# Two-layer adaLN block on one core: each attention maximum placed behind the next reciprocal of row 0's Sinkhorn chains

## The chip, the cores and the metric

The kernel runs on one core of one Trainium2 chip. A core has five engines that work side by side, each from its own list of instructions and in the order of that list: TensorE (PE; PEld is its weight load), VectorE (DVE), ScalarE (ACT), GpSimd (POOL) and SyncE (SP), which here issues the DMAs. An instruction that waits for another engine holds up everything behind it in its own list. The metric is the time of one execution on the device in microseconds, the median of several.

## The reference

Two transformer layers work on `x` of shape (2, 512, 512): two rows (batch entries, `b`) of 512 tokens. Each layer normalises, modulates, runs an attention, then normalises, modulates and runs a second part. Layer 0 is a large gated linear attention (32 heads of 128) and a binarised matrix product; it takes the first 850 us and the change does not touch it. Layer 1 is a softmax attention with 32 heads of 16, and after it a mixing of four streams of 128 channels whose 4x4 mixing matrix comes from a Sinkhorn iteration:

```python
def step(carry, _):
    u, v = carry
    u = -jax.nn.logsumexp(Z + v[..., None, :], axis=-1)
    v = -jax.nn.logsumexp(Z + u[..., :, None], axis=-2)
    return ((u, v), None)
(u, v), _ = jax.lax.scan(step, (u0, v0), None, length=50)
H_res = jnp.exp(Z + u[..., :, None] + v[..., None, :])
```

A token has 16 logits `Z`; 50 iterations of a row step and a column step follow each other, every step a function of the one before. The softmax of the attention is `softmax(q k / 4)` over 512 keys, and its result is added to `x` before the mixing reads it.

## The kernel before

Tokens lie 128 to a tile, so a row has four tiles and there are eight in all.

Attention of layer 1. It is cut into 16 groups (`order`, two rows x two halves of the queries x four head groups), each in 8 pieces. `piece()` runs through them. For each piece `maxima` makes two maxima: a matmul of scores for 128 queries by 512 keys into a PSUM buffer (L880; the pool `s1` has three) and a reduction to the row's negated maximum on VectorE (L884). After four pieces' share of them (8 maxima) the maxima are split in a high and a low part (L894 on ScalarE, L895 on GpSimd), turned on TensorE (L898) and written by a DMA (L904) as extra rows of the queries. Some ten pieces later `weigh` computes the scores again in the turned layout, with the maximum subtracted inside the matmul (L918), and ScalarE takes the exponential (L78, `pt`). `outputs` multiplies by the values (L938), `finish` turns, divides and adds to `x` (L960, L964, L966 and on GpSimd L972). There are 256 maxima, numbered 0 to 255 here.

Sinkhorn chains. When a quarter of the tokens (half a row, two tiles) has its attention, a generator for its mixing goes onto the list `side`, which `piece()` advances by two steps a piece (`aside(2)`). For row 0 that is `streams0(0)` and `streams0(2)`: `opening` (normalisation and logits), `first_iteration`, 49 further `iterations` and the mixing. For row 1 `streams1a` runs 16 iterations of the first half, `streams1b` then opens the second half, runs 33 iterations of both halves together ("joint") and 16 more of the second half alone.

A chain keeps `K = exp(Z + u + v)` and two factors `fa` and `fb`. A half iteration multiplies `K` by one factor, sums over four, and takes the reciprocal:

- row 0: the product (L1183 or L1187) and the sum in two additions (L1176, L1177) on GpSimd, the reciprocal (L1185 or L1189) on VectorE, 98 reciprocals a chain;
- row 1 (`last` is true): product, sum (L1173) and reciprocal all on VectorE, 130 reciprocals.

At iterations 16 and 32 of a run (`RENEW`) the factors are folded into `u` and `v` and `K` is computed anew (L1193, L1166, L1167 on VectorE, logarithms and the exponential on ScalarE). At the end `result` forms the matrix (L1200, L1201, L1204), ScalarE makes diagonal matrices of its entries (L1215), TensorE mixes (L1236), and `put` scales and adds (L1210 on VectorE, L1211 on GpSimd) and stores.

Order. The order of each engine's list is not the order of the text. A scheduler places every instruction by priorities (`tc.high_priority` moves work forward) and by its own estimate of when operands are ready. `tc.add_manual_dep(a, b, order_only)` adds a rule: `a` stands behind `b` in their engine's list; where both are on one engine it puts no semaphore between them. In the resulting list VectorE had 64 of the first chain's 98 reciprocals, 28 of the second's and 2 of row 1's 130 ahead of the last maximum.

Of the kernel before, what the change touches and what calls it, by code (L numbers as in the profile page):

```python
# [52 lines left out]
def tile_adaln(ctx: ExitStack, tc: tile.TileContext, a: dict, out: bass.AP):  # L53
    nc = tc.nc
# [22 lines left out]
    def act(o, i, func, **kw):  # L77
        ins = nc.scalar.activation(o, i, func, **kw)  # L78
        tc.add_manual_dep(
            ins.ins, table.ins.name,  # L80
            mybir.DependencyInfo(mybir.DependencyClass.NoSync, mybir.DependencyReason.DATA),
            reason="the activation table",
        )
        return ins.ins
# [52 lines left out]
    anchor = {}  # L137
    order_only = mybir.DependencyInfo(mybir.DependencyClass.NoSync, mybir.DependencyReason.DATA)
# [32 lines left out]
    def temp(shape, dt, name, bufs=2):  # L171
        return wk.tile(shape, dt, name=name, bufs=bufs)
# [642 lines left out]
    def key_tile(i):  # L815
        return i % 2 if i < TWO else (i - TWO + 2) % 3
# [54 lines left out]
    def maxima(st, k):  # L871

        assert holder[key_tile(st["i"])] == st["i"]
        rp, j = divmod(k, 4)
        s, i = divmod(j, 2)
        if j == 0:
            st["m"] = small.tile([P, NQ * 2, 2], FP, name="m")
        for qt in range(NQ):
            ps = psp.tile([P, L], FP, name="s1", bufs=S1)
            anchor["pe"] = nc.tensor.matmul(  # L880
                ps, lhsT=st["qs"][rp][0:KS, i, qt * P:(qt + 1) * P], rhs=st["ks"][s][0:KS],
                start=True, stop=True,
            ).ins
            anchor["dve"] = nc.vector.tensor_reduce(  # L884
                st["m"][:, 2 * qt + s, i:i + 1], ps, AX.X, ALU.max, negate=True
            ).ins
        if j == 3:
            m2 = small.tile([P, NQ * 2, 2, 2], FR, name="m2")
            hi, lo = m2[:, :, 0], m2[:, :, 1]
            if st is order[-1]:  # L890
                nc.vector.tensor_copy(hi, st["m"])
                nc.vector.tensor_tensor(lo, st["m"], hi.bitcast(FP), ALU.subtract)
            else:
                nc.scalar.copy(hi, st["m"])  # L894
                nc.gpsimd.tensor_tensor(lo, st["m"], hi.bitcast(FP), ALU.subtract)  # L895
            mt = psp.tile([8, Q], FP, name="mt", bufs=MT)
            for qt in range(NQ):
                nc.tensor.transpose(  # L898
                    mt[:, qt * P:(qt + 1) * P],
                    m2[:, 2 * qt:2 * qt + 2].bitcast(FP).rearrange("p a b c -> p (a b c)"), ident,  # L900
                )
            mm = temp([8, L], FR, "mm")[:, 0:Q]
            nc.scalar.copy(mm, mt)
            anchor["sp"] = nc.sync.dma_start(out=st["qs"][rp].bitcast(FP)[96:100], in_=mm.bitcast(FP)).ins  # L904

    def weigh(st, k):

        assert holder[key_tile(st["i"])] == st["i"]
        rp, r = divmod(k, 4)
        kp, s = divmod(r, 2)  # L910
        if r == 0:
            quads.append({"st": st, "rp": rp, "pt": {}})
        qd = quads[-1]
        for i in range(2):
            ps = psp.tile([P, 2, Q], FP, name="s2", bufs=S2)
            for j in range(2):
                kt = 2 * kp + j
                nc.tensor.matmul(  # L918
                    ps[:, j, :], lhsT=st["ks"][s][0:KM, kt * P:(kt + 1) * P], rhs=st["qs"][rp][0:KM, i, :],
                    start=True, stop=True,  # L920
                )
            p = wts.tile([P, 2, Q], FP, name="pt", bufs=PT)
            anchor["act"] = qd["last"] = act(p, ps, AF.Exp, scale=0.25)
            qd["pt"][2 * s + i, kp] = p

    quads = []

# [232 lines left out]
    def iterations(R, its, renew, last):  # L1160

        z, t, K, u, v, fa, fb, fl = (R[k] for k in ("z", "t", "K", "u", "v", "fa", "fb", "fl"))
        big = nc.vector if last else nc.gpsimd

        def kernel_of():
            nc.vector.tensor_tensor(K, z, over(u), ALU.add)  # L1166
            nc.vector.tensor_tensor(K, K, along(v), ALU.add)  # L1167
            act(K, K, AF.Exp)

        def sums(dst, y):  # L1170

            if last:
                nc.vector.tensor_reduce(dst, y, AX.X, ALU.add)  # L1173
            else:
                h2 = R["pairs"]
                nc.gpsimd.tensor_tensor(h2, y[:, :, :, 0:2], y[:, :, :, 2:4], ALU.add)  # L1176
                nc.gpsimd.tensor_tensor(dst, h2[:, :, :, 0], h2[:, :, :, 1], ALU.add)  # L1177

        for it in its:
            if it == 1 or it - 1 in renew:  # L1180
                sums(fa, K)
            else:
                big.tensor_tensor(t, K, along(fb), ALU.mult)  # L1183
                sums(fa, t)
            nc.vector.reciprocal(fa, fa)  # L1185
            yield
            big.tensor_tensor(t, tp_(K), along(fa), ALU.mult)  # L1187
            sums(fb, t)
            nc.vector.reciprocal(fb, fb)  # L1189
            if it in renew:  # L1190
                for d, f in ((u, fa), (v, fb)):
                    act(fl, f, AF.Ln)
                    nc.vector.tensor_tensor(d, d, fl, ALU.add)  # L1193
                kernel_of()
            yield
# [70 lines left out]
    def streams0(c0):  # L1266

        S = {"b": 0, "c0": c0, "n": 2}
        yield from opening(S, False)
        R = chain_room(2, False)  # L1270
        yield from first_iteration(S, R)
        yield from S["branch"]
        yield from iterations(R, range(1, NITER), RENEW, False)
        result(S, R)
        for c in range(2):
            yield from mixed_on_tensor(S, c, nc.gpsimd)
# [3 lines left out]
    def streams1a():  # L1280

        S = joint["a"] = {"b": 1, "c0": 0, "n": 2}
        yield from opening(S, True)
        R = joint["R"] = chain_room(4, True)
        yield from first_iteration(S, part(R, 0, 2))
        yield from S["branch"]
        yield from iterations(part(R, 0, 2), range(1, HEAD + 1), (HEAD,), True)

    def streams1b(ahead):
# [16 lines left out]

        side.append((1, branches(), UP))
        yield from iterations(R, range(1, NITER - HEAD), RENEW, True)
        result(A, part(R, 0, 2))
        side.append((None, mixed_on_tensor(A, 0, nc.gpsimd), UP))  # L1310
# [44 lines left out]
    def piece():  # L1355
        p = at[0]
        at[0] += 1
        if p == 0:
            begin()
        i, k = divmod(p, 8)  # L1360
        if k == 0 and i < len(order):
            load_step(i + 1)
        if p < n_pieces:
            maxima(order[i], k)
        if wt[0] <= p - slack(p):
            weighed()
        if k == 4 and i + 1 < len(order):
            keys1(i + 1)
        with tc.high_priority(UP):
            if p >= HOLD and p % POP == 0 and virtual:  # L1370
                tail(virtual.pop(0))
        aside(2)
# [3 lines left out]
    def weighed():  # L1376
        w = wt[0]
        wt[0] += 1
        if w < n_pieces:
            if w == n_pieces // 2:  # L1380
                values1(1)
            weigh(order[w // 8], w % 8)
        o = w - OUT
        if 0 <= o < n_pieces and o % 4 == 3:
            outputs(o // 4)
        o -= 5
        if o >= 0 and o % 4 == 0 and o < n_pieces:
            j = o // 4
            finish(j)
            if j % 16 == 5:  # L1390
                with behind():
                    row_tiles(j // 16, (SB, CB, GB))
                    weights24(j // 16)
            if j % 8 == 7:
                k = j // 8
                if k == 2:
                    joint["ahead"] = streams1a()
                side.append((RATES[k], (streams0(2 * k) if k < 2 else joint["ahead"] if k == 2 else streams1b(joint["ahead"])), UPS[k]))
# [40 lines left out]
    for n, u in enumerate(units):  # L1439
        g, b, c = u["at"]  # L1440
        s = n // NC
# [127 lines left out]
```

## Time and profile before

| | us |
|---|---|
| median of 3 runs (1355.14 to 1362.71) | 1359.68 |
| profiled execution | 1362.77 |
| its span | 1361.1 |
| first and last maximum start | 854.6, 1224.4 |
| first chain of row 0: first and last reciprocal | 1081.1, 1275.7 |
| second chain of row 0: first and last reciprocal | 1159.1, 1323.4 |
| row 1's chain: first and last reciprocal | 1217.0, 1347.2 |

Over the span TensorE is busy 91%, VectorE 81%, ScalarE 62% and GpSimd 58%; the mean granted clock of TensorE is 0.961. In the lines that follow, a row of stages gives for each engine the busy time and the number of instructions, then the granted clock of TensorE (PEclk), the share of the DMA engines and what they moved. A row of the timeline gives start, length, engine, line, operation, what is written and read, and the count. A group gives busy time, mean length of one in ns, and after the second bar the idle time ahead of them and what ended it.

### The profile page before, as it was taken

The numbers are of one execution on the slowest core, as the hardware profiler recorded it, in microseconds if no ns is written. First come the engines' busy times: TensorE is split into PE (matmuls) and PEld (weight loads), VectorE is DVE, ScalarE is ACT, GpSimd is POOL, SyncE is SP. The second block draws the span as 40 slices with busy tenths as digits, with TensorE's granted clock in tenths as the row PEclk, the third lists the DMA queues.
The fourth block names the chain that finished last, engine by engine and source line by source line (L and its number), as shares of the span: only waits on it lengthen the run. The fifth ranks groups of instructions, "written<-read, shape, count | busy, mean of one in ns | idle before, by whom it ended". The sixth has DMA issues, their size and how long they took to land. (4 is left out here: it accounts for less than half of the span.)

```text
span 1361.1 us, 23047 instructions
## 1 busy us (share of the span) xinstructions
PE 1236.3 (91%) x7216; PEld 996.9 (73%) x7216; DVE 1098.5 (81%) x2668; ACT 845.2 (62%) x2380; POOL 788.3 (58%) x1235
## 2 busy tenths in 40 slices
PE   6889999999999999999989999898999999995408
PEld 3677888788788778888877787676777777764308
DVE  7897678787686687877989887867878888898888
ACT  4565476476466566766657675566667678775417
POOL 5353374365266357776788878444444755668751
PEclk9999999999999999999999999998998999997659
DMA  8111341231132142333343233424203221200001
GB/s 255 57 57 32 97 121 40 71 109 55 46 95 93 54 139 95 86 108 93 101 125 109 82 113 91 127 71 132 81 28 116 81 68 50 66 14 2 9 8 47
DMA packets 69762, 109.68 MB, mean 81 GB/s; under 512 B 13436, under 2 KB 20348, under 8 KB 69640
## 3 DMA queue, kind: packets, MB, share of 16 engines
q1 hardware_dynamic: 69640, 108.21, 26.9%
q8 instruction: 57, 0.93, 0.3%
q14 instruction: 65, 0.53, 0.1%
HBM read 99.89 MB, written 8.02 MB: 79 GB/s over the span
## 5 line engine op out<-in xcount | busy, mean ns | idle before, releaser
L884 DVE TENSOR_REDUCE m<-s 128x1 f32<-128x512 f32 x256 | 165.7, 670 | 13.6 <-PE s L880 13.0
L78 ACT ACTIVATE pt<-s 128x512 f32<-128x512 f32 x256 | 137.6, 600 | 13.4 <-PE s L918 12.6
L78 ACT ACTIVATE sg<-sg 128x512 f32<-128x512 f32 x128 | 80.8, 632 | 57.9 <-DVE sg L512 56.0
L481 POOL TENSOR_TENSOR q<-xcos,rot 128x512 f32<-128x512 f32 x64 | 92.9, 1452 | 39.7 <-DVE xcos L479 36.9
L880 PE MATMUL s<-ks,qs 96*128 96x512 f32 x256 | 105.1, 438 | 8.4 <-DVE m L884 6.2
L251 PE MATMUL pps<-hh,wq_h 128*128 128x512 f32 x256 | 102.0, 399 | 0.9 <-DVE zl L605 0.9
L78 ACT ACTIVATE dec<-dec,room 128x128 f32<-128x128 f32 x256 | 82.7, 398 | 32.1 <-POOL dec L529 31.9
L529 POOL TENSOR_SCALAR_AFFINE_SELECT dec<-gb 128x512 f32<-128x512 f32 x64 | 47.1, 736 | 95.6 <-DMA gb<-g_dram 35.1
L251 PE MATMUL ops<-wo_h,zh 128*128 128x512 f32 x256 | 101.3, 396 | 0.9 <-DVE zl L605 0.9
L251 PE MATMUL ops<-wo_h,zl 128*128 128x512 f32 x256 | 100.8, 394 | 0.9 <-DVE zl L605 0.9
L251 PE MATMUL gps<-wg_h,hh 128*128 128x512 f32 x256 | 101.1, 395 | 0.0
L251 PE MATMUL gps<-wg_l,hh 128*128 128x512 f32 x256 | 101.0, 394 | 0.0
L918 PE MATMUL s<-qs,ks 100*128 100x256 f32 x512 | 99.3, 301 | 1.7 <-ACT pt L78 1.2
L251 PE MATMUL gps<-wg_h,hl 128*128 128x512 f32 x256 | 100.6, 393 | 0.0
L251 PE MATMUL pps<-hl,wq_h 128*128 128x512 f32 x256 | 100.3, 392 | 0.0
L251 PE MATMUL ops<-wo_l,zh 128*128 128x512 f32 x256 | 100.1, 391 | 0.0
L251 PE MATMUL pps<-hh,wq_l 128*128 128x512 f32 x256 | 100.1, 391 | 0.0
L549 POOL TENSOR_TENSOR gb<-gb,q 128x512 f32<-128x512 f32 x48 | 63.2, 1318 | 63.1 <-ACT gb L78 52.2
L582 PE MATMUL yps<-v,dec 128*128 128x128 f32 x512 | 93.8, 278 | 3.8 <-DVE xcos L479 2.8
L918 PEld LDWEIGHTS s<-qs,ks 100*128 100x128 f32 x512 | 83.0, 195 | 18.0 <-ACT pt L78 5.3
L592 DVE SCALAR_TENSOR_TENSOR z<-yps,ss,sg 128x128 f32<-128x128 f32 x256 | 71.8, 341 | 28.4 <-ACT ss L78 28.1
L556 POOL TENSOR_TENSOR xw<-v,room 128x512 f32<-128x512 f32 x48 | 55.5, 1171 | 60.4 <-ACT v L496 58.1
(327 smaller groups left out, 3924.5 us busy)
## 6 DMA issues: line engine op xcount, KB each, us to landing
gb<-g_dram SPq DMA_DIRECT2D x64, 256.0 KB
raw<-in_wq SPq DMA_DIRECT2D x56, 256.0 KB
raw<-in_wg SPq DMA_DIRECT2D x48, 256.0 KB
raw<-in_wo SPq DMA_DIRECT2D x48, 256.0 KB
raw<-in_wmod SPq DMA_DIRECT2D x40, 256.0 KB
qs<-q_dram SPq DMA_DIRECT2D x64, 64.0 KB
raw<-in_wk SPq DMA_DIRECT2D x14, 256.0 KB
raw<-in_wv SPq DMA_DIRECT2D x14, 256.0 KB
```

What stands on the lines that cost most here:

```text
L78: ins = nc.scalar.activation(o, i, func, **kw)
L251: nc.tensor.matmul(ps, lhsT=l, rhs=r, start=i == 0, stop=i == n - 1)
L481: nc.gpsimd.tensor_tensor(dst, sp(xc_), sp(rot), ALU.add)
L529: anchor["pool"] = nc.gpsimd.affine_select(out=dec, in_=gb, pattern=[[0, REP0], [1, P]], compare_op=ALU.is_ge, fill=-1e30, base=0, channel ...
L549: nc.gpsimd.tensor_tensor(gb, gb, q[:, c], ALU.mult)
L556: nc.gpsimd.tensor_tensor(xw, u["v"][:, c, :].unsqueeze(1).to_broadcast(sh4), wdc[:, c, r0:r0 + REP0].unsqueeze(2).to_broadcast(sh4), ALU. ...
L582: nc.tensor.matmul(yps[:, h, :], lhsT=u["pr"][:, h, :], rhs=u["v"][:, c, :], start=True, stop=not c)
L592: nc.vector.scalar_tensor_tensor(z[:, h, :], yps[:, h, :], ss[:, h:h + 1], sg[:, h * P:(h + 1) * P], ALU.mult, ALU.mult)
L880: anchor["pe"] = nc.tensor.matmul(ps, lhsT=st["qs"][rp][0:KS, i, qt * P:(qt + 1) * P], rhs=st["ks"][s][0:KS], start=True, stop=True,).ins
L884: anchor["dve"] = nc.vector.tensor_reduce(st["m"][:, 2 * qt + s, i:i + 1], ps, AX.X, ALU.max, negate=True).ins
L918: nc.tensor.matmul(ps[:, j, :], lhsT=st["ks"][s][0:KM, kt * P:(kt + 1) * P], rhs=st["qs"][rp][0:KM, i, :], start=True, stop=True,)
```

## The change

Every reciprocal of a chain that has its products on GpSimd is noted in `paced`, a list for each chain. When a maximum is emitted, `pace` takes the next noted reciprocal from each list and demands that the maximum stand behind it. A rule concerns the order of VectorE's list alone. Nothing else is edited; the scheduler places all instructions anew under these rules.

```diff
             anchor["dve"] = nc.vector.tensor_reduce(
                 st["m"][:, 2 * qt + s, i:i + 1], ps, AX.X, ALU.max, negate=True
             ).ins
+            pace(anchor["dve"])
...
+    paced = {}
+
+    def pace(m):
+
+        for q in paced.values():
+            if q:
+                tc.add_manual_dep(m, q.pop(0).name, order_only, reason="the chain's reciprocals keep pace")
...
-            nc.vector.reciprocal(fa, fa)
+            r = nc.vector.reciprocal(fa, fa).ins
+            if not last:
+                paced.setdefault(id(R), []).append(r)
             yield
             big.tensor_tensor(t, tp_(K), along(fa), ALU.mult)
             sums(fb, t)
-            nc.vector.reciprocal(fb, fb)
+            r = nc.vector.reciprocal(fb, fb).ins
+            if not last:
+                paced[id(R)].append(r)
```

The lines behind the edits move: L884 stays, L1183, L1185, L1187 and L1189 become L1192, L1194, L1198 and L1200, L1176 and L1177 become L1185 and L1186.

## The prediction

> **What bounds the kernel now.** I read the page first (TensorE busy 91% of the span), then the busy time by stages, because the change touches only the last 280 us:
>
> ```profile
> core 0: us, PE busy (x) PEld busy (x) DVE busy (x) ACT busy (x) POOL busy (x), PEclk, DMA share, GB/s
> 1100.00:1120.00 20.00, 20.00 (x194) 14.79 (x190) 16.96 (x45) 15.33 (x35) 9.62 (x42) 1.00 0.18 50
> 1242.00:1256.00 14.00, 3.10 (x18) 2.74 (x18) 12.80 (x84) 4.58 (x17) 12.36 (x53) 0.57 0.00 1
> 1256.00:1276.00 20.00, 3.92 (x16) 3.25 (x15) 17.86 (x100) 3.55 (x13) 17.26 (x90) 0.50 0.00 0
> 1300.00:1324.00 24.00, 0.00 (x0) 0.00 (x0) 21.04 (x111) 0.69 (x3) 13.86 (x61) 0.50 0.00 1
> ```
>
> The attention (maxima until 1224.4) is bound by TensorE: PE is busy 20.00 of 20 us. After it PE is all but idle, and VectorE works through row 1's Sinkhorn chain, with row 0's two chains on GpSimd (POOL) between its instructions. The groups of 1100 to 1200 give the attention's pace:
>
> ```profile
> L884 DVE TENSOR_REDUCE m<-s 128x1 f32<-128x512 f32 x110 | 70.6, 666 | 9.3 <-PE s L880 9.0
> ```
>
> 110 maxima in 100 us, 0.91 us each. Next the timeline inside the attention, one half iteration of row 0's first chain (L1185 and L1189 are the reciprocals, L1187, L1176, L1177 its three GpSimd steps, L884 a maximum):
>
> ```profile
> 1152.05 0.19 DVE L1185 RECIPROCAL sinkhorn<-sinkhorn 128x8 f32<-128x8 f32 x1
> ...
> 1152.24 0.64 DVE L884 TENSOR_REDUCE m<-s 128x1 f32<-128x512 f32 x1
> 1152.32 0.25 POOL L1187 TENSOR_TENSOR sinkhorn<-sinkhorn 128x32 f32<-128x32 f32 x1
> ...
> 1152.65 0.22 POOL L1176 TENSOR_TENSOR sinkhorn<-sinkhorn 128x16 f32<-128x16 f32 x1
> ...
> 1152.95 0.20 POOL L1177 TENSOR_TENSOR sinkhorn<-sinkhorn 128x8 f32<-128x8 f32 x1
> 1152.97 0.68 DVE L884 TENSOR_REDUCE m<-s 128x1 f32<-128x512 f32 x1
> ...
> 1153.77 0.68 DVE L884 TENSOR_REDUCE m<-s 128x1 f32<-128x512 f32 x1
> ...
> 1154.37 0.19 DVE L1189 RECIPROCAL sinkhorn<-sinkhorn 128x8 f32<-128x8 f32 x1
> ```
>
> GpSimd is done at 1153.15, but the reciprocal stands behind two more maxima and starts at 1154.37: a half iteration takes 2.32 us here, and the chain is late, not the attention. The same steps with no maxima about, from the timeline of the tail, when row 0's second chain is alone on GpSimd:
>
> ```profile
> 1302.66 0.20 DVE L1189 RECIPROCAL sinkhorn<-sinkhorn 128x8 f32<-128x8 f32 x1
> ...
> 1303.55 0.20 POOL L1177 TENSOR_TENSOR sinkhorn<-sinkhorn 128x8 f32<-128x8 f32 x1
> ...
> 1303.79 0.20 DVE L1185 RECIPROCAL sinkhorn<-sinkhorn 128x8 f32<-128x8 f32 x1
> ...
> 1304.93 0.20 DVE L1189 RECIPROCAL sinkhorn<-sinkhorn 128x8 f32<-128x8 f32 x1
> ```
>
> 1.13 and 1.14 us; (1307.30 - 1302.66) / 4 = 1.16 over four. That is the chain's own speed, and it is slower than the 0.91 us of a maximum.
>
> **The change, part by part.** No instruction is added or removed. Each maximum gets the next reciprocal of each chain then at hand ahead of it in VectorE's list. Counted in the two built orders: of the first chain's 98 reciprocals, 64 stood ahead of the last maximum, now all 98; of the second's 98, 28, now 97; of row 1's 130, 2, now 23. Maxima 96 to 159 alternate one to one with the first chain, 160 to 191 with both, 192 to 255 with the second. VectorE takes its list in order, so a maximum now waits for GpSimd. Behind it wait the matmuls L880 that need its PSUM buffer (three), behind those in PE's list the scores L918 and outputs L938, and then ScalarE's exponentials: the whole attention falls to the chain's pace.
>
> (1) The pace. 128 steps with one chain at 1.16 us are 148.5. With two chains the tail shows the first chain's L1189 at 1262.32 and again at 1272.98, eight half iterations later: 1.33 us; 32 steps are 42.6. Together 191 us. A maximum itself (0.65) and the small VectorE work fit between two reciprocals, and PE's 0.91 lies inside the 1.16; both cost nothing as long as the step is longer. Bounds: 1.13 a step (the shortest row) below; above, 1.41 and 1.50, the means inside the attention (29 half iterations of the first chain from 1100 to 1160, and 27 of the second from 1160 to 1225) from a reciprocal's start to the end of its last sum, with GpSimd's other work included. I take 1.16 and 1.33 and list that other work:
>
> (2) Head: six GpSimd steps of row 1's rotary work (L702, L708) stand between the first half iterations; reciprocals 2 to 4 were at 1082.25, 1087.06 and 1091.08, so about 6 us over two normal steps. (3) The second chain's opening puts four 128x512 operations on GpSimd (L1061, L1062: 2.8 and 2.5 us); the half iteration over them took 5.9 us (1137.9 to 1143.80), 4.5 over a step. (4) Renewals: two in each chain; reciprocal 1148.19 to 1152.05 is 3.9, about 1 of it behind maxima, so 1.7 over a step; four make 7. (5) Every 8 maxima GpSimd adds an output (L972, 0.46) and a remainder (L895, 0.20): 20 x 0.66 = 13, half of it in the chain's own waits: 6. (6) Row 1's first 21 half iterations now stand among the last 25 maxima, some 0.6 us of VectorE a step beside 0.72 for maximum and reciprocal; 1.4 in place of 1.16: 7. (7) The first chain's mixing (40 diagonals on ScalarE at 0.29, two L1210 at 0.7, two adds on GpSimd) now lies among maxima 192 to 204: 4. Sum of 2 to 7: 34.5; from half of it to all.
>
> The first reciprocal was at 1081.07, with maxima 96 to 101 ahead of it; they now stand behind it, and four of them stood in the first iteration: about 1079. So the last maximum starts at 1079 + 191 + 34.5 = 1304.5, where it was at 1224.4: +80.
>
> (8) The tail. From the last maximum to row 1's joint iterations 31 us pass (1224.4 to 1256), set by the last exponentials, the last outputs and the second half's opening; it stays. But the second chain's mixing, 40 diagonals of 0.29 = 12 us of ScalarE, moves from 1324 into this drain, where ScalarE was busy 15.8 of 22 us, and its L1210 stands on VectorE ahead of the last outputs: +9 (0 if ScalarE finds room, 12 if not). Then row 1's 66 joint half iterations took 1256 to 1322.4 = 66.4 us beside row 0's chains; alone one is 0.80 (reciprocals at 1280.58 and 1281.38, while the second chain waits for a renewal): 53, and 5 for the joint chain's own two renewals, so -8, the stalls on row 0's results at 1284 to 1291 included. The tail is +1, between -15 (no drain, and every joint step at the 0.70 of the narrower steps after 1324) and +5.
>
> Reorderings of at most 36 places in the first 100 us come from the scheduler; the work is the same and PE is full there (100.00 of 100): 0, within 3. SP's list moves by at most 10 places (the last stores by 31); its queue loads L846 and copies L904 are the same number, spread over a longer stage, with the DMA share at 0.18: 0.
>
> Sum: +80 + 1 = +81. The profiled execution took 1362.8 (span 1361.1), 3.1 above the median 1359.68 of the runs shown; so 1362.8 + 81 - 3.1 = 1441.
>
> At this pace PE is busy about 0.91 / 1.4 = 65%. The rows show what can happen to its clock: 0.57 granted where PE was busy 22%, 1.00 where 85% (1220 to 1242), 0.96 at 60% (the last 14 us), 0.82 in 1081 to 1100. I take 1.00: at 0.8 PE's 0.91 becomes 1.14 at most and still lies inside the step.
>
> [...]
>
> **The rivals.**
> Not slower: the chain keeps pace with the attention because a waiting reciprocal was all that slowed it. For it: 23 of the first chain's 29 half iterations from 1100 to 1160 lose 0.4 us or more behind maxima. Then the last maximum stays at 1224 and the tail gives -8 to +1: 1352 to 1361. It decides where the 160 steps end 8 us late at most, (1232 - 1079) / 160 = 0.96 us a step; the shortest way from a reciprocal through GpSimd to the next is 1.13 in the rows shown, so I give it 2%.
> Cheap: the extras hide in each other and the tail gains its full 15. 128 x 1.13 + 32 x 1.25 + 17 = 202, last maximum at 1279: +55 - 15 = +40, 1400. For it: many extras are single waits that VectorE's slack can take.
> Dear: waits add up because each list is in order on five engines and two stand in a loop (the remainder L895 waits for ScalarE, which waits for maxima): 128 x 1.41 + 32 x 1.50 + 24 = 252, PE late 10: last maximum at 1341, +117, tail +5: 1482. A cooled PE belongs here.
> Nothing happens: the order shows that the lists differ; only an attention that waits for something else at 1.2 us anyway would hide it, and PE at 100% speaks against that.
>
> **How the numbers follow.** Forecast (1415 to 1465): 0.61. Cheap (1383 to 1415): 0.16. Dear (above 1465): 0.19. Not slower: 0.02. Nothing: 0.02. The range takes in most of cheap and dear: 1396 to 1485. Faster by over 0.5% 0.02, within 0.5% (what a measurement of this kernel can tell from no change) 0.02, slower 0.96.
>
> **What would show it.** The last maximum between 1280 and 1340; the attention's maxima at 1.2 to 1.5 us each; idle time before L1194 and L1200 (the reciprocals' new lines) put down to GpSimd's L1186, in place of few us now; PE busy 60 to 75% from 1100 on; no reciprocal of row 0's chains later than 5 us after the last maximum; 66 joint half iterations in 56 to 62 us. It is wrong if maxima run faster than 1.1 us, which a GpSimd part under 1 us would need, or if the tail shrinks by more than 20.

## The result, and the profile after

The changed kernel takes 1440.68 us (median of 6 runs, 1439.24 to 1442.68) where the kernel before takes 1360.23 (6 runs, 1355.14 to 1362.71): 1.0592 times as long, 95% interval 1.0571 to 1.0614. Its profiled execution took 1440.46, with a span of 1438.7, so 77.6 us more span than before.

The page of the kernel after: the span, the granted clock of TensorE in 40 slices (36 us each), and the group of the maxima (count, busy time and mean of one, then the idle time of VectorE ahead of them).

```profile
span 1438.7 us, 23052 instructions
...
PEclk9999999999999999999999999999998778988656
...
L884 DVE TENSOR_REDUCE m<-s 128x1 f32<-128x512 f32 x256 | 165.3, 659 | 10.1 <-PE s L880 10.1
```

Up to 1079 us the digit is 9 (0.9 or more) in every slice; from there to 1295 it is 7 or 8 in all but one of six. The busy time by stages of the kernel after (length, then busy time and instructions of each engine, granted clock, DMA share, GB/s):

```profile
core 0: us, PE busy (x) PEld busy (x) DVE busy (x) ACT busy (x) POOL busy (x), PEclk, DMA share, GB/s
1074.30:1311.10 236.80, 196.17 (x1401) 130.35 (x1405) 168.52 (x570) 132.76 (x340) 155.87 (x648) 0.84 0.12 35
...
1311.00:1345.00 34.00, 23.00 (x228) 18.26 (x220) 18.33 (x78) 22.37 (x69) 7.13 (x11) 0.89 0.04 16
1345.00:1401.00 56.00, 7.94 (x44) 7.20 (x44) 48.24 (x214) 9.74 (x36) 0.00 (x0) 0.56 0.00 1
```

The first row is the stretch from maximum 96 to the last one, 255. The same stretch of the kernel before:

```profile
1062.90:1224.40 161.50, 158.10 (x1370) 118.67 (x1370) 144.33 (x424) 122.73 (x302) 101.67 (x354) 0.98 0.22 59
```

161.5 us became 236.8. The stretch also begins 11.4 us later than in the kernel before, since maximum 96 now stands behind the first chain's first reciprocal, and what follows the last maximum is 9.1 us shorter: 11.4 + 75.3 - 9.1 = 77.6. TensorE's matmuls in the stretch are nearly the same (1401 and 1370), but it was short of work for 40.6 us of it (3.4 before), and was busy 38 us longer with them, at a mean clock of 0.84 in place of 0.98. No engine is full any more: the 159 maxima stand 1.49 us apart. In the last row GpSimd has nothing left: row 0's chains are done, and row 1's joint half iterations run alone. Two of these, from the timeline of the kernel after:

```profile
1349.51 0.25 DVE L1200 RECIPROCAL sinkhorn<-sinkhorn 128x16 f32<-128x16 f32 x1
1350.31 0.25 DVE L1194 RECIPROCAL sinkhorn<-sinkhorn 128x16 f32<-128x16 f32 x1
```

0.80 us. Below, the timeline of the kernel after where maxima and the first chain alternate:

```profile
1106.33 0.20 DVE L1194 RECIPROCAL sinkhorn<-sinkhorn 128x8 f32<-128x8 f32 x1 [0.60 <-POOL sinkhorn L1186]
1106.45 0.64 DVE L884 TENSOR_REDUCE m<-s 128x1 f32<-128x512 f32 x1
1106.61 0.25 POOL L1198 TENSOR_TENSOR sinkhorn<-sinkhorn 128x32 f32<-128x32 f32 x1 [0.32 <-DVE sinkhorn L1194]
...
1107.23 0.20 POOL L1186 TENSOR_TENSOR sinkhorn<-sinkhorn 128x8 f32<-128x8 f32 x1
1107.46 0.20 DVE L1200 RECIPROCAL sinkhorn<-sinkhorn 128x8 f32<-128x8 f32 x1 [0.38 <-POOL sinkhorn L1186]
1107.58 0.64 DVE L884 TENSOR_REDUCE m<-s 128x1 f32<-128x512 f32 x1
```

One half iteration, 1.13 us, and one maximum in it. The maximum is done at 1107.09; VectorE then idles 0.38 us for GpSimd's second addition, and the next maximum stands behind that. The waits of the kernel after between 1074 and 1311 (engine and line, what it waited for, us in total, times, longest):

```profile
DVE sinkhorn L1194 <- POOL sinkhorn L1186: 24.7, 49, 2.6
DVE sinkhorn L1200 <- POOL sinkhorn L1186: 23.1, 50, 2.1
...
PE s L880 <- DVE m L884: 15.6, 24, 2.1
PE s L919 <- DMA qs<-mm: 11.2, 10, 2.4
DVE m L884 <- PE s L880: 9.1, 8, 2.1
```

The same waits in the kernel before between 1081 and 1224:

```profile
DVE m L884 <- PE s L880: 11.2, 14, 1.8
...
DVE sinkhorn L1185 <- POOL sinkhorn L1177: 3.7, 6, 1.1
...
PE s L880 <- DVE m L884: 1.0, 3, 0.4
...
DVE sinkhorn L1189 <- POOL sinkhorn L1177: 0.2, 1, 0.2
```

The two waits for L1186 are the forecast's: 47.8 us, where the kernel before has 3.9 (6.4 over its whole span). The third line shows how the attention falls to the chain's pace: TensorE's scores wait for the maxima, 15.6 us for 1.0. The last two lines of the kernel after were not in the forecast as a cost: TensorE waits for a DMA, and VectorE then waits for TensorE. VectorE waited for TensorE no less in the kernel before (11.2 us), where TensorE was the bound; now such a wait also holds up the chain.

The stretch was taken apart by following each reciprocal to the next: the way from its start to the end of its second addition on GpSimd, what GpSimd's other work adds to the usual way, and by how much the next reciprocal starts later than that addition allows ("VectorE late").

| | forecast | measured |
|---|---|---|
| stretch begins (first reciprocal) | 1079 | 1074.3 |
| usual way: 64 x 1.10, 32 x 1.23, 63 x 1.11, and 0.03 each | 191 | 184.6 |
| GpSimd's other work | 34.5 | 28 |
| VectorE late | 0 | 20.6 |
| not put down | 0 | 3.6 |
| last maximum starts | 1304.5 | 1311.1 |
| from there to the joint iterations (31.8 before) | 40 | 34.2 |
| 66 joint half iterations (65.4 before) | 58 | 56.1 |
| rest of the span (39.5 before) | as before | 37.3 |

Where VectorE is late, TensorE mostly was late first. The timeline of the kernel after, 1093 to 1103:

```profile
1096.44 1.62 PE L919 MATMUL s<-qs,ks 100*128 100x256 f32 x6 [1.10 <-DMA qs<-mm]
...
1098.42 3.64 PE L947 MATMUL op<-pt,va 128*32 128x256 f32 x32
...
1100.83 0.20 DVE L1200 RECIPROCAL sinkhorn<-sinkhorn 128x8 f32<-128x8 f32 x1 [0.93 <-POOL sinkhorn L1186]
...
1101.99 1.03 PE L880 MATMUL s<-ks,qs 96*128 96x512 f32 x3
...
1102.59 0.69 DVE L884 TENSOR_REDUCE m<-s 128x1 f32<-128x512 f32 x1 [1.55 <-PE s L880]
```

The second scores (L919) wait for the transfer that brings their maxima (`qs<-mm`). Then 32 output matmuls (L947) take 3.64 us, the scores of the next maximum (L880) stand behind them, and that maximum comes 1.55 us late. The next reciprocal is behind it in VectorE's list. That part of the order is the scheduler's own: the new rule only asks that a maximum stand behind its reciprocal, and here one reciprocal more than it asks for runs ahead of the late maximum before the chain, too, has to wait. The clock ahead of this and during it, from the busy times of the kernel after:

```profile
1088.50:1095.30 6.80, 5.32 (x27) 3.49 (x27) 4.08 (x15) 4.08 (x10) 3.60 (x16) 1.00 0.29 88
...
1095.30:1102.10 6.80, 5.70 (x41) 3.07 (x40) 3.31 (x10) 1.57 (x3) 3.96 (x18) 0.50 0.03 11
```

The clock was halved for 75 us of the 236.8, in ten pieces of 3.4 to 13.7 us (one of 6.8 us before).

### The profile page after: what moved, and what is told of

Its sections match the earlier page's. It is cut to its first block, busy times and chain, and to the rows that moved or that the text cites. A ratio compares the mean times of both kernels' runs of the same rounds, so it can differ in the third digit from the quotient of the medians.

```text
span 1438.7 us, 23052 instructions
## 1 busy us (share of the span) xinstructions
PE 1272.8 (88%) x7216; PEld 1003.9 (70%) x7216; DVE 1113.3 (77%) x2668; ACT 846.5 (59%) x2380; POOL 790.4 (55%) x1235
## 4 chain that ended last, share of the span: by engine, by line
PE 67%; DVE 13%; ACT 6%; POOL 5%; DMA 5%; issue 4%; SPq 1%; ACTq 0%; POOLq 0%; DVEq 0%
PE pps L251 17%; PE ops L251 11%; PE gps L251 10%; PE op L947 4%; PE yps L582 3%; PE sps L251 3%; PE s L919 3%; PE s L880 3%; PE yps L584 3%; ACT pt L78 2%; PE cps L251 2%; PE mix L1249 2%; PE ztp L600 2%; PE mps L290 1%; DMA qs<-mm 1%
## 5 line engine op out<-in xcount | busy, mean ns | idle before, releaser
L884 DVE TENSOR_REDUCE m<-s 128x1 f32<-128x512 f32 x256 | 165.3, 659 | 10.1 <-PE s L880 10.1
L880 PE MATMUL s<-ks,qs 96*128 96x512 f32 x256 | 114.0, 474 | 26.2 <-DVE m L884 20.6
L919 PE MATMUL s<-qs,ks 100*128 100x256 f32 x512 | 101.7, 313 | 12.8 <-DMA qs<-mm 11.2
L919 PEld LDWEIGHTS s<-qs,ks 100*128 100x128 f32 x512 | 83.5, 205 | 31.7 <-issue 9.8
L1249 PE MATMUL mix<-h,dg 128*128 128x128 f32 x224 | 36.0, 312 | 63.3 <-ACT dg L1228 63.2
```

Of the source, the lines that this page charges most:

```text
L880: anchor["pe"] = nc.tensor.matmul(ps, lhsT=st["qs"][rp][0:KS, i, qt * P:(qt + 1) * P], rhs=st["ks"][s][0:KS], start=True, stop=True,).ins
L884: anchor["dve"] = nc.vector.tensor_reduce(st["m"][:, 2 * qt + s, i:i + 1], ps, AX.X, ALU.max, negate=True).ins
L919: nc.tensor.matmul(ps[:, j, :], lhsT=st["ks"][s][0:KM, kt * P:(kt + 1) * P], rhs=st["qs"][rp][0:KM, i, :], start=True, stop=True,)
L1249: nc.tensor.matmul(mps[:, i], lhsT=dg[:, j], rhs=hv[:, j] if j < NS else yb[:, c], start=n > NS and j == 0, stop=j == n - 1 and (n > NS or ...
```

## The experiments

**The theory:** the one-to-one order makes the attention run at the chain's step, so the loss is (a) the step's length over TensorE's pace, and (b) every single wait of either side, which the order hands to the other. **The rivals:** the loss is mainly something else that came with the new order (TensorE late through the transfers and its clock; the tail; row 0's mixing), or it follows simply from how many reciprocals stand ahead of the maxima.

**A longer step.** One more GpSimd operation in each half iteration of row 0's chains, which changes no value. First in the kernel after, then the same line in the kernel before, where the chains have time.

```diff
                 nc.gpsimd.tensor_tensor(dst, h2[:, :, :, 0], h2[:, :, :, 1], ALU.add)
+                nc.gpsimd.tensor_scalar(dst, dst, 1.0, 0.0, ALU.mult, ALU.add)
```

> One more dependent GpSimd operation (128x8, times one) in every half iteration of row 0's chains, in the changed kernel. Theory (the attention runs at the chain's pace): a dependent GpSimd step of this size is about 0.30 us from start to start, so single-chain steps go from 1.14 to 1.44 and two-chain steps from 1.27 to about 1.6: 128 x 0.30 + 32 x 0.35 = +49, last maximum at about 1360 where it was at 1311, end at about 1490. Rival (the lists were merely reshuffled, and the attention loses its time to other waits): the same as in the kernel before with the same operation, under +15.

> The same added GpSimd operation in the kernel before, as a control. Theory: the attention does not wait for the chain, so the last maximum stays at 1224 within 5 us; in the tail the second chain has 70 half iterations left and row 1's chain shares a list with them, so the end moves by +10 to +30. Rival: no difference between this and the changed kernel's rise.

Measured (one run each): in the kernel after 1468.63, beside 1363.62 for the kernel before on that chip. The timeline of this kernel (L1187 is the added operation):

```profile
1110.11 0.20 DVE L1201 RECIPROCAL sinkhorn<-sinkhorn 128x8 f32<-128x8 f32 x1 [0.67 <-POOL sinkhorn L1187]
...
1111.29 0.20 POOL L1187 TENSOR_SCALAR sinkhorn<-sinkhorn 128x8 f32<-128x8 f32 x1
1111.52 0.20 DVE L1195 RECIPROCAL sinkhorn<-sinkhorn 128x8 f32<-128x8 f32 x1 [0.66 <-POOL sinkhorn L1187]
```

The step is 1.41 here, some 0.29 longer (0.36 where both chains run), and over the stretch that would be 48 us, as expected. Yet the stretch grew by 30.4 only (236.8 to 267.2), and the end came 21 us below the 1490 expected: the lateness of VectorE fell from 20.6 to 8.7 us, as would follow if a longer step hides more of TensorE's; some 6 us of the difference were not put down. So the step sets the pace, and VectorE's lateness stands in addition to it.

In the kernel before the same line cost 20 us (1383.87), and none of it in the attention: the last maximum started at 1221.1 (1224.4). The second chain ended at 1343.1 (1323.4), and the end moved with it: row 0's mixing starts when that chain ends, with row 1's diagonal matrices behind it in ScalarE's list. GpSimd's step is free for the attention where nothing is locked to it.

**A shorter step.** Two ways: the sum over two of four terms with one addition, and row 0's reciprocals taken of a constant, while the sums go to another tile.

```diff
-                nc.gpsimd.tensor_tensor(h2, y[:, :, :, 0:2], y[:, :, :, 2:4], ALU.add)
-                nc.gpsimd.tensor_tensor(dst, h2[:, :, :, 0], h2[:, :, :, 1], ALU.add)
+                nc.gpsimd.tensor_tensor(dst, y[:, :, :, 0], y[:, :, :, 2], ALU.add)
```

> The changed kernel with one GpSimd addition in a half iteration where there were two: a sum takes two of the four terms, so the matrix is another (part of the computation is left out). Theory: a half iteration alone falls to about 0.84 us, under the 0.91 us that TensorE needs for a maximum, so the attention is bound by TensorE again, apart from single waits of 15 to 20 us: last maximum at about 1250, end at about 1378. Rival (reshuffled lists): the end stays above 1425.

```diff
-                nc.gpsimd.tensor_tensor(dst, h2[:, :, :, 0], h2[:, :, :, 1], ALU.add)
+                nc.gpsimd.tensor_tensor(R["sum"], h2[:, :, :, 0], h2[:, :, :, 1], ALU.add)
...
-            r = nc.vector.reciprocal(fa, fa).ins
+            r = nc.vector.reciprocal(fa, fa if last else R["one"]).ins
...
-            r = nc.vector.reciprocal(fb, fb).ins
+            r = nc.vector.reciprocal(fb, fb if last else R["one"]).ins
```

> The changed kernel with row 0's reciprocals taken of a constant, so that they no longer need the sum of their own half iteration (the matrix is another: that part of the computation is left out); the rule on the order and all instructions stay. The reciprocal still waits for GpSimd to have read the factor one half iteration earlier. Theory: the way GpSimd to VectorE and back leaves the step, GpSimd's three operations of 0.85 us alone remain, under TensorE's 0.91, while two chains still take 1.27: last maximum at about 1255, end at about 1380. Rival (order itself costs the time): end above 1425.

Measured (one run each): 1399.12 and 1403.48 (before 1363.62), some 20 us above what was expected of both and below the 1425 of the rival. The timeline of the kernel with the short sum:

```profile
1098.06 0.20 DVE L1199 RECIPROCAL sinkhorn<-sinkhorn 128x8 f32<-128x8 f32 x1
1098.34 0.24 POOL L1191 TENSOR_TENSOR sinkhorn<-sinkhorn 128x32 f32<-128x32 f32 x1 [0.32 <-DVE sinkhorn L1199]
1098.66 0.20 POOL L1185 TENSOR_TENSOR sinkhorn<-sinkhorn 128x8 f32<-128x8 f32 x1
1098.89 0.20 DVE L1193 RECIPROCAL sinkhorn<-sinkhorn 128x8 f32<-128x8 f32 x1
```

A step of 0.83 is below TensorE's 0.91 for a maximum; over the stretch the median step is 0.91. If only the step's length cost time, the stretch should be that of before, 161.5 us. It is 196.2, and 205.0 with the constant. So of the 75.3 us that the change added to the stretch, 40.6 go with the step (a), and about 35 stay when the step is as short as TensorE's own (b). The expectation of the first run had 15 to 20 us for (b). The granted clock was 0.95 with the shorter step, where the kernel after has 0.84; the stretch of the kernel with the short sum:

```profile
1073.30:1269.50 196.20, 172.75 (x1405) 121.08 (x1409) 158.95 (x548) 131.04 (x340) 115.62 (x449) 0.95 0.15 42
```

It was halved for 20.5 us there, where the kernel after has 75. A block of 32 outputs takes 1.93 us at the full clock and 3.64 at the halved one (kernel after, from 1107.1 and from 1098.4); by that, an estimate, half of 20.5 is the most that the halved clock added to TensorE's work, some 10 of the 35 us that stay. Of the 40.6, on the other hand, a part can be the clock's: no run holds it fixed.

**Fewer locked pairs.** The pace rule for every second maximum alone, for three of four, and for the first chain alone.

```diff
+    count = [0]
     def pace(m):
+        count[0] += 1
+        if count[0] % 2:
+            return
```

> Only every second maximum takes a reciprocal of each chain ahead of it. Theory: two maxima to a chain step of 1.14 (or 1.27) need 1.82 us of TensorE, so the chain is no longer the bound: last maximum at 1225 to 1240, fewer reciprocals in the tail (13 of the first chain and 50 of the second where 34 and 70 were left), end at 1345 to 1365, ratio to the kernel before 0.99 to 1.005. Rival (any such rule reshuffles the lists and costs): above 1390.

In the second kernel the condition is `count[0] % 4 == 0`.

> Three of four maxima take a reciprocal of each chain ahead of them. Theory: the chain asks 0.86 us a maximum alone and 0.95 with two chains, beside TensorE's 0.91, so the mean fits but single waits (head, opening, renewals) are no longer hidden: last maximum at about 1245, end at 1360 to 1390. Rival: the loss falls in proportion to the share of paced maxima, three quarters of 80: 1420.

```diff
-        for q in paced.values():
+        for q in list(paced.values())[:1]:
```

> Only the first chain's reciprocals pace the maxima, so maxima 192 to 255 are free. Theory: maxima 96 to 191 at the chain's 1.14 with its waits as in the changed kernel (maximum 192 at about 1215, where it was 1222.5), the last 64 at 0.92: last maximum at about 1274, end at 1395 to 1410. Rival (the loss sits where both chains or row 1's chain meet the maxima): under 1375 or above 1425.

| rule for | reciprocals ahead of the last maximum (first, second, row 1's chain) | time, us | ratio to before | stretch, us |
|---|---|---|---|---|
| none (before) | 64, 28, 2 | 1360.23 | 1 | 161.5 |
| every second maximum | 85, 48, 8 | 1379.01 | 1.0137 (1.0118 to 1.0155) | 183.4 |
| three of four | 98, 73, 21 | 1415.15 | 1.0407 (1.0375 to 1.0439) | 210.7 |
| every maximum, first chain | 98, 59, 5 | 1412.72 (one run; before 1359.66) | 1.039 | 207.7 |
| every maximum (after) | 98, 97, 23 | 1440.68 | 1.0592 (1.0571 to 1.0614) | 236.8 |

The half rule was expected to cost nothing: two maxima to a step leave TensorE 1.8 us for a step of 1.15. It cost 1.4%, 22 us of stretch. The timeline shows one place where; the kernel with the half rule, at the second chain's opening:

```profile
1137.26 0.20 DVE L1204 RECIPROCAL sinkhorn<-sinkhorn 128x8 f32<-128x8 f32 x1
...
1139.69 2.87 POOL L1074 TENSOR_TENSOR h<-h,row 128x512 f32<-128x512 f32 x2
1142.69 2.50 POOL L1075 TENSOR_TENSOR h<-h,row 128x512 f32<-128x512 f32 x2
...
1145.81 0.20 DVE L1198 RECIPROCAL sinkhorn<-sinkhorn 128x8 f32<-128x8 f32 x1 [1.33 <-POOL sinkhorn L1190]
```

This half iteration took 8.5 us, since four large operations of GpSimd (5.4 us) and a renewal stand in it, and the paired maxima stood behind it: five maxima start in these 8.5 us. Being fast on the mean does not help: with fixed pairs, no maximum may run ahead while GpSimd is away. For three of four, the rival that goes by the number of pairs expected 1420 and is the nearer, against 1360 to 1390; by the same proportion the half rule would have taken 1400, where it took 1379. The first chain's rule came within 3 us of what the theory expected, with the last maximum at 1281.8: its last 64 maxima, with nothing to pace them, took 64.8 us.

**TensorE's share of the single waits.** Is the halved clock the cause? One try gives TensorE more work: each matmul of the second scores is done twice, with the same result. It was run on the kernel after, and as a control on the kernel before.

```diff
+                nc.tensor.matmul(
+                    ps[:, j, :], lhsT=st["ks"][s][0:KM, kt * P:(kt + 1) * P], rhs=st["qs"][rp][0:KM, i, :],
+                    start=True, stop=True,
+                )
```

> The changed kernel with each matmul of the second scores (512 of 256 columns) done twice into the same place. It adds about 0.24 us of TensorE at the full clock to a maximum, 1.15 in all beside the chain's step of 1.14 and its waits. Theory: TensorE has that room in the changed kernel and its clock, at half for 68 of the 237 us, stays up: end between 1430 and 1455. Rival (TensorE, cooled, is what sets the step): +37 and more, above 1475.

> The kernel before with each matmul of the second scores done twice, as a control to the same edit in the changed kernel, whose end it moved by 31 us (1440.7 to 1471.9). Theory now: in the kernel before TensorE has no idle time in the attention, so all of the added work lands: 256 maxima of 0.24 us, some 60 us over the whole attention of layer 1, of which 154 x 0.24 = 37 after maximum 96; end 1400 to 1425. In the changed kernel only a part of the 37 landed, because a step of the chain hides some of TensorE's work. Rival (TensorE limits the changed kernel as much as the kernel before): the rise here is 31 or less.

Measured (one run each): 1471.89 (before 1359.66) for the kernel after, above what the theory expected and 3 us below the rival's bound; 1402.97 (before 1361.60) for the kernel before, within what was expected. (The expectation's 68 us of halved clock in the kernel after are 75 by its trace.) The stretch of each, from the busy times, first with the doubled scores in the kernel after:

```profile
1084.20:1341.10 256.90, 224.62 (x1758) 171.93 (x1760) 169.37 (x568) 138.77 (x344) 158.35 (x644) 0.89 0.12 35
```

and in the kernel before:

```profile
1068.30:1263.70 195.40, 192.93 (x1687) 154.13 (x1686) 157.07 (x495) 130.05 (x309) 125.84 (x485) 1.00 0.17 48
```

In the kernel before TensorE is full, so the doubled work shows whole: 33.9 us. In the kernel after 20.1 of that show, although TensorE has 40 us to spare there on the mean. The added matmuls raised VectorE's lateness from 20.6 to about 35 us. So "it fits into the step" is not true of TensorE's work in single steps: the group of the maxima of this kernel between 1100 and 1200 shows 14.4 us of idle time for TensorE where the kernel after shows 4.3. The group of this kernel, then that of the kernel after:

```profile
L884 DVE TENSOR_REDUCE m<-s 128x1 f32<-128x512 f32 x63 | 40.7, 648 | 14.4 <-PE s L880 14.4
L884 DVE TENSOR_REDUCE m<-s 128x1 f32<-128x512 f32 x69 | 44.3, 646 | 4.3 <-PE s L880 4.3
```

The halved time fell to 58 us with the added work, but this does not tell the clock's share apart: the work itself cost more.

The other try takes away the wait for the transfer. Counted in the traces, the second scores stand mostly 5 to 8 pieces behind the maxima in the kernel after, 6.5 to 11 in the kernel before and 4 to 11 under the half rule. A rule holds them back behind the maxima's scores at hand; 11 pieces result.

```diff
-                nc.tensor.matmul(
+                mm = nc.tensor.matmul(
...
-                )
+                ).ins
+                tc.add_manual_dep(mm, anchor["pe"].name, order_only, reason="behind the scores at hand")
```

> The changed kernel with one more rule of order on TensorE: the second scores stand behind the maxima's scores of the piece at hand, so they keep 11 pieces behind the maxima (the scheduler had let them come up to 4 to 7 pieces, where the kernel before had 8 to 11). Theory now: TensorE's waits for the DMA that brings back the turned maxima (1.9 us each) and the halved clock after them, which makes the outputs 3.6 us long and the next maximum late, are 15 to 25 of the attention's 75 us; they go: last maximum at 1285 to 1298, time in halved clock under 40 us, end 1415 to 1430. Rival (the single waits are GpSimd's and the chain's own alone): end within 5 of 1440.

> The same rule with every second maximum paced. Theory now: there the second scores were 6.5 to 11 pieces behind, so only a part of the 22 us by which that attention is longer than the kernel before comes from TensorE's waits: 5 to 10 go, end 1369 to 1375; the rest is single waits of the chain (head, opening, renewals) passed on by the fixed order. Rival (all of the 22 us is TensorE's waits): 1357 or less.

> The same rule in the kernel before, as a control: there TensorE is busy without a break and the second scores are 6.5 to 11 pieces behind already. Theory: within 6 us of the kernel before, either way. Rival (the rule speeds the attention by itself): 10 or more below.

| the rule added to | time, us | before on that chip | ratio | stretch, us (without it) |
|---|---|---|---|---|
| after | 1436.01 | 1359.39 | 1.0550 (1.0511 to 1.0590) | 226.7 (236.8) |
| the half rule | 1388.05 | 1359.39 | 1.0202 (1.0170 to 1.0234) | 190.1 (183.4) |
| before | 1368.53 | 1359.39 | 1.0060 (1.0043 to 1.0078) | 167.6 (161.5) |

In the kernel after the rule took away the wait. TensorE's waits from 1074 to 1311 have no line of a DMA `qs<-mm` any more, and the wait for the maxima, 15.6 us without the rule, is now 20.4:

```profile
PE s L880 <- DVE m L884: 20.4, 30, 3.1
```

VectorE's lateness fell from 20.6 to about 11.5 us, and the stretch by 10.1. The 32 outputs, in the chain of waits of this kernel,

```profile
1121.38 1.86 PE op L948 x32
```

take 1.86 us (granted clock 0.96 from 1113 to 1124), against 3.57 in the chain of waits of the kernel after (0.50 from 1095.3 to 1102.1):

```profile
1094.36 1.95 DMA qs<-mm
...
1098.49 3.57 PE op L947 x32
```

But the gain in the time is 5 us, not the 15 to 25 that were expected, and 1436 lies where the rival had it: the stretch began 7.5 us later. The halved time fell from 75 to 58 us and not below 40. The control shows that the rule itself costs 9 us in the kernel before, where at most 6 had been expected, and about as much with the half rule, where a gain had been expected. If it costs as much in the kernel after, which no run shows, it is worth some 14 us there. Of the 35 us of single waits, then, some 10 by the stretch, and 14 on that assumption, come from TensorE's transfer waits and what follows from them; the rest was not put down to single causes.

None of these kernels is faster than the kernel before: from the last maximum to the end it takes 136.7 us, the kernels with a pacing rule 126 to 133, so pacing gives back 11 us at most, and the half rule's stretch alone costs 22.

## Why the prediction was right

**The pace (1)** was right. The step is 1.13 to 1.16 with one chain, medians of 1.14 and 1.27 were measured, and the usual way made 184.6 us for the 191 of the sum. That it is the step, and not the number of pairs alone, was shown by the longer sum (30.4 us more stretch with nearly the same pairs) and by the shorter one (40.6 us less).

**The sentence in (1) that failed** is that maximum, small VectorE work and TensorE's 0.91 "lie inside" the step and cost nothing. They cost 20.6 us. Seven tenths of that, by the trace, pass while VectorE is in or waits for a maximum or an output that TensorE brought late (10.3 of 14.5 us on the first chain, 7.2 of 10.6 on the second, each followed over its whole course, so that the part where both run counts twice); the rest is VectorE's own work, such as row 1's rotary products ahead of the third reciprocal. The mean hid it: 0.91 fits into 1.16, but with the halved clock TensorE was busy 196.17 / 159 = 1.23 us a maximum, and a block of 32 outputs took 3.64 us in one piece.

**The clock** was taken as 1.00; 0.84 was granted. The side sentence that at 0.8 the 0.91 "becomes 1.14 at most and still lies inside the step" is the same error, a mean put against a step. That the clock would be full with TensorE busy 65% was the author's estimate and shown by no run: in the stretch it was halved ten times, 75 us together, with TensorE busy 83%.

**GpSimd's other work (2 to 7)** was 28 us for 34.5. The opening's half iteration took 5.6 us, 4.5 over a step, against 4.5 (the 5.9 of the kernel before are 4.7 over 1.16); the four renewals' 1.7 to 2.8 us each, some 4.5 over their steps, against 7; the half iteration with the mixing 3.9, 2.7 over, against 4. Row 1's half iterations among the last maxima did not show as a term of their own: the last 31 maxima stood 1.35 us apart, less than the mean.

**The start** was 1074.3 and not 1079: maximum 96 went directly behind the first reciprocal.

**The tail (8)** was -9.1 us for +1. The 66 joint half iterations gave 9.3 (forecast 8; in the kernel before they had taken 65.4 us, one step less than the 66.4 that the prediction read). The drain grew by 2.4, not 9: ScalarE, busy 22.37 of 34 us there, found room for most of the second chain's mixing.

So the errors were of both signs: +20.6 and +3.6 in the stretch, -4.7, -6.4 and -6.5 on its other terms, and -10.1 in the tail, some -3.5 together; 81 were forecast and 77.6 came. The path was right, but that the time came within 1 us of 1441 is luck: four errors of 5 to 10 us one way met 24 us the other way, and the 3.1 us taken off for a profiled execution above the median were not needed, since the changed kernel's lay on its median.

**The rivals.** (In the prediction's sum for "cheap", 1079 + 202 is 1281, not 1279, so 1402.) "Not slower" needed 0.96 us a step; even a step of 0.91 left the short sum at 1399. "Cheap" and "Dear" each had a true half: the tail's gain was of cheap's kind, and the late TensorE at a lower clock ("cooled" in the prediction) was named in dear. Of the signs named, one was wrong for the attention: TensorE was busy 83% there and not 60 to 75%, as the slower clock stretched the same work (the 158.1 us of the kernel before would be 67% of the 236.8). The last reciprocal of row 0 came at 1312.0, 0.8 us behind the last maximum.

**Open.** How much of the 20.6 us, and of the 75.3 us of the stretch, the halved clock costs by itself, apart from the transfer waits that come with it, was not separated. The runs also leave open whether the 7.5 us ahead of the stretch in the kernel with held scores come from that rule alone.

## What to carry to other kernels

Before two lists are locked one to one, put the round trip of the one (here 1.13 us through GpSimd) against the pace of the other (0.91): the slower sets both. A pair that would win on the mean still loses, because a fixed order passes each single wait on (a large operation on the shared engine, a late transfer) to the other side, which used to run ahead of it. And "it fits into the step" is to be shown block by block, by the longest piece that stands between two steps, not by a mean.

## What the runs showed of the hardware

- TensorE's granted clock was 0.84 over the stretch of the kernel after. By its trace the clock was halved ten times in these 236.8 us, for 75 us together, though TensorE was busy 83% of them and its longest idle gap was 2.6 us. The stretches of other runs, busy share of TensorE and granted clock: the longer sum 80% and 0.81; the scores held back 84% and 0.87; the scores doubled 87% and 0.89; the short sum 88% and 0.95; the kernel before 98% and 0.98, and with its scores doubled 99% and 1.00. What makes the clock fall or come back, and whether the busy share moves the clock or the clock the busy share, these runs do not show.
- A round trip from VectorE through three dependent GpSimd operations of 8 to 32 elements a partition and back took 1.13 us (kernel after, 1106.33 to 1107.46), one more operation 0.29 (some 1.41 us with the longer sum, 1110.11 to 1111.52), and one less with a smaller add 0.30 less (0.83 with the short sum, 1098.06 to 1098.89). Two chains that alternate on the two engines took 1.27 a step (median, kernel after).
